# Scan rows ordered so that neighbours on DVE do not depend on each other, statistics aggregated among the rows, and the last stage's weights loaded and folded during the scan

## The chip, the cores and the metric

One NeuronCore of a Trainium2 chip. Its engines each run their own list of instructions in order and wait for one another through semaphores: PE (matrix products and transposes, into the PSUM memory), DVE (vector arithmetic), ACT (scalar engine: copies, scaling, functions; it can also issue DMAs), POOL (a second, slower vector engine without access to PSUM) and SP (issues DMAs). PEld is PE's weight load. The metric is the time on the device of one execution, in microseconds (us).

## The reference

Four layers, each of the form x + f(groupnorm(x)), on x of 4 images x 128 x 128 pixels x 128 channels in float32; a norm group is 4 channels of an image.

```python
x = x + relu(deform_conv(gn(x), w_off, b_off, w_def))     # layer 0: 3x3, bilinear samples
# layer 1: a scan over 128 rows, each row of 128 pixels
def step(carry, row):
    new = row + relu(conv1d_same(carry, W))               # 9 taps, 128 -> 128 channels
    return (new, new)
x = x + scan(step, gn(x))
z = gn(x)                                                 # layer 2
x = x + z @ Wself.T + (sum(z, 2) @ Wm.T)[:, :, None] + (sum(z, 1) @ Wk.T)[:, None]
xn = layer_norm(gn(x))                                    # layer 3: a triangle product
left, right = (xn @ lw + lb) * sigmoid(xn @ lgw + lgb), (xn @ rw + rb) * sigmoid(xn @ rgw + rgb)
out = einsum('bkjd,bkid->bijd', left, right)
x = x + (layer_norm(out) * sigmoid(xn @ ogw + ogb)) @ to_out_w + to_out_b
```

Layer 1 is the serial part: row y + 1 needs the finished row y. Below, x1 is the result of layer 0 and x2 that of layer 1.

## The kernel before

Three stages follow one another: `deform_layer` (layer 0), `scan_layer` (layer 1) and `message_and_triangle` (layers 2 and 3). Inside each main part the order of every engine's list is the order in which the code is written (`manual_schedule`); the framework adds the semaphore waits that the data and the reuse of buffers call for.

**Between layer 0 and the scan.** `deform_layer` ends with what is left of the last convolution, 32 `bn_stats` on the last chunk of x1, the groupnorm factors of the last image (`x1_norm`), and then a flag `far` (L757 to L769): whether any sampling offset left a small window. `ranges` holds the offsets' extremes. After it the program branches on `far`; all five engines read the flag, branch and meet again. The general path isn't taken with these inputs.

**The scan.** The four images go side by side. A row's pixels are split by position modulo 3 into three phases of 43, 43 and 42 columns, and the nine-tap convolution is done as a short convolution over the phases, which saves products: `carry` holds three phases (parts 0 to 2) and three sums of them (parts 3 to 5): 0+1, 1+2, 0+1+2. In each row PE makes the `edge` product (L1081, `pa`: two weights, first with carry part 0, then with part 2), then four products `m1` (part 1), `m01` (part 3), `m12` (part 4) and `m012` (part 5), each in its own PSUM bank, and then it transposes row y + 1 (`turned`, L1061). ACT copies `m1` out of PSUM (L1111) and scales the transposed row with the norm (`scaled`, L1068, `rowT`). DVE then works down one chain: `e = m01 - m1` (L1117), `y0 = edge + e` (L1119), carry part 0 = max(y0, 0) + rowT (L1120), `f = m12 - m1` (L1124), `y2 = f - edge` (L1127), carry part 2 (L1128), `e + f` (L1131), `y1 = m012 - (e + f)` (L1133), carry part 1 (L1134), the three sums of carries (L1141 to L1143), three additions of x1 into `x2c` (L1145), and four `bn_stats`, one for each image (L1150). POOL adds x2 over the rows (`sum_h`, L1148); SP stores four rows at a time to x2T (L1153) and loads four rows of x1 at a time (L1052). PSUM is full: two banks for the transposed rows (`ps_x`), two for the edge products, four for the others.

After the last row DVE computes `sum_w` from the statistics and then aggregates 128 rows of statistics for each image (L1157, `counted`).

**The start of the last stage.** `message_and_triangle` loads its weights: the square matrices and columns on ACT's queue (L1196 to L1230), five bias rows on SP's (L1227, L1231). The norm's gain and the removal of the mean are folded into `wcat`, the 640 columns of all five projections, by two products with `less` and `first` for each of two column blocks (L1244, L1247). Then SP fetches the first two blocks of x2T into `R` (L1342). `prelude(0)` turns `counted` into the group factors (a product with `gmean`, the variance, another product, a square root on ACT at L86, a reciprocal on DVE), and makes the message terms. Then `sums_of(0)` multiplies R into `self_ps` (L1354) and writes `X` (L1365).

Of the kernel before, what the change touches and what calls it, by code (L numbers as in the profile page):

```python
# [9 lines left out]
F32 = mybir.dt.float32  # L10
# [8 lines left out]
P = 128  # L19
B = 4  # L20
# [12 lines left out]
DQ = P // NQ  # L33

# [145 lines left out]
def deform_layer(tc, c, small, x, w_off, b_off, w_def, x1, tabs, offs):  # L180
# [14 lines left out]
    with ExitStack() as ctx:  # L195
# [552 lines left out]
        for _ in convs:  # L748
            pass
        count(len(to_count))  # L750
        beside["norms"].append(x1_norm(B - 1, stats))
        while step(B, S):
            pass


# [4 lines left out]
        nc.vector.scalar_tensor_tensor(most, ends[:, 1:2], -1.0, ends[:, 0:1], ALU.mult, ALU.max)  # L760
        most_ps = ps_g.tile([1, 2 * NL], F32, name="most_ps", tag="gn_ps")
# [7 lines left out]
        nc.vector.tensor_copy(far, row)  # L769
        return norms, far  # L770
# [240 lines left out]
def scan_layer(tc, c, small, x1, w, norms, x2T):  # L1011
# [4 lines left out]
    WP = N + 5  # L1016
    counted = small.tile([P, B, 2], F32, name="counted2")
    sum_w = small.tile([P, B, S], F32, name="sum_w")
    sum_h = small.tile([P, B, S], F32, name="sum_h")
    with ExitStack() as ctx:  # L1020
# [5 lines left out]
        ps_m = ctx.enter_context(tc.tile_pool(name="l1ps_m", bufs=1, space=PSUM))  # L1026

        stats = wp.tile([P, B, S, 6], F32, name="stats2")
# [14 lines left out]

        carry = [wp.tile([P, 2 * PHASES, B, WP], F32, name=f"carry_{i}") for i in range(2)]
# [40 lines left out]

        order = {getattr(mybir.EngineType, e) for e in ("PE", "Activation", "DVE", "Pool", "SP")}
        ctx.enter_context(tc.manual_schedule(engines=order))
        chunks = {0: rows(0), RB: rows(RB)}
        px = turned(0)
        ready = {0: (px, scaled(px))}  # L1090
        add, less = ALU.add, ALU.subtract
        for y in range(S):
# [7 lines left out]
            if y:  # L1100
# [10 lines left out]
                nc.scalar.copy(m1, ps["m1"])  # L1111
            if y + 1 < S:
                pn = turned(y + 1)
                ready[y + 1] = (pn, scaled(pn))
            if y:
                e = two.tile([P, B, N], F32, name="e")
                nc.vector.tensor_tensor(e, ps["m01"], m1, less)  # L1117
                y0 = two.tile([P, B, N], F32, name="y0")
                nc.vector.tensor_tensor(y0, pa[:, :, 0:N], e, add)  # L1119
                nc.vector.scalar_tensor_tensor(  # L1120
# [3 lines left out]
                nc.vector.tensor_tensor(f, ps["m12"], m1, less)  # L1124
                y2 = two.tile([P, B, N], F32, name="y2")
                n2 = COUNT[2]
                nc.vector.tensor_tensor(y2[:, :, 0:n2], f[:, :, 0:n2], pa[:, :, 1 : 1 + n2], less)  # L1127
                nc.vector.scalar_tensor_tensor(  # L1128
                    kept(new, 2), y2[:, :, 0:n2], 0.0, part(rt, 2), ALU.max, add
                )  # L1130
                nc.vector.tensor_tensor(e, e, f, add)  # L1131
                y1 = two.tile([P, B, N], F32, name="y1")
                nc.vector.tensor_tensor(y1, ps["m012"], e, less)  # L1133
                nc.vector.scalar_tensor_tensor(  # L1134
# [5 lines left out]
            if y + 1 < S:  # L1140
                nc.vector.tensor_tensor(kept(new, 3, N), kept(new, 0, N), kept(new, 1, N), add)  # L1141
                nc.vector.tensor_tensor(kept(new, 4, N), kept(new, 1, N), kept(new, 2, N), add)
                nc.vector.tensor_tensor(kept(new, 5, N), kept(new, 3, N), kept(new, 2, N), add)  # L1143
            for p in range(PHASES):
                nc.vector.tensor_tensor(  # L1145
                    x2c[:, :, i, p:S:PHASES], part(px, p), kept(new, p), add
                )
            nc.gpsimd.tensor_tensor(sum_h, sum_h, x2c[:, :, i], add)  # L1148
            for b in range(B):
                nc.vector.bn_stats(stats[:, b, y, :], x2c[:, b, i])  # L1150
# [3 lines left out]
        nc.vector.tensor_tensor(sum_w, stats[:, :, :, 1], stats[:, :, :, 4], add)  # L1154
        nc.vector.tensor_scalar(sum_w, sum_w, S / 2.0, None, ALU.mult)
        for b in range(B):
            nc.vector.bn_aggr(counted[:, b], stats[:, b].rearrange("p n s -> p (n s)"))  # L1157
# [17 lines left out]
def message_and_triangle(tc, c, x2T, x3d, gates, counted, w2, w3, out):  # L1175
# [5 lines left out]
    wself_T, wm_T, wk_T = w2  # L1181
    (norm_g, norm_b, left_w, left_b, right_w, right_b, lgate_w, lgate_b, rgate_w, rgate_b,
     ogate_w, ogate_b, onorm_g, onorm_b, to_out_w, to_out_b) = w3
# [7 lines left out]
    with ExitStack() as ctx:  # L1191
        wp = ctx.enter_context(tc.tile_pool(name="l3w", bufs=1))

        def column(v, name):
            t = wp.tile([P, 1], F32, name=name)
            nc.scalar.dma_start(t, v.rearrange("(p o) -> p o", o=1))  # L1196
            return t

        wself = wp.tile([P, P], F32, name="wself")
        nc.scalar.dma_start(wself, wself_T)  # L1200
        wm = wp.tile([P, P], F32, name="wm")
        nc.scalar.dma_start(wm, wm_T)
        wk = wp.tile([P, P], F32, name="wk")
        nc.scalar.dma_start(wk, wk_T)
        gcol = column(norm_g, "gcol")
        bcol = column(norm_b, "bcol")
        og = column(onorm_g, "og")
        ob = column(onorm_b, "ob")
        outb = column(to_out_b, "outb")
        outw = wp.tile([P, P], F32, name="outw")  # L1210
        nc.scalar.dma_start(outw, to_out_w)

        wcat = wp.tile([P, NW + P], F32, name="wcat")
        with tc.tile_pool(name="l3prep", bufs=1) as prep, tc.tile_pool(
            name="l3ps_w", bufs=2, space=PSUM
        ) as ps_w:
            raw = prep.tile([P, NW + P], F32, name="wraw")  # L1220
            braw = prep.tile([1, NW + P], F32, name="braw")
# [540 lines left out]
```

## Time and profile before

| what | value |
|---|---|
| median of 3 runs | 5691.27 us (5687.96 to 5703.16) |
| the profiled execution | 5688.34 us, its span 5686.6 us |
| layer 0, until the engines branch | 0 to 3336 us |
| branch and start of the scan | 3336 to 3354 us |
| the scan's rows | 3354 to 4098 us |
| end of the scan, prelude | 4098 to 4142 us |
| the last stage | 4142 to 5686 us |
| PE busy over the span | 5214.1 us, 92% |
| DVE busy over the span | 3277.2 us, 58% |
| ACT busy over the span | 2798.5 us, 49% |

How to read it: a line of the timeline gives the start in us, the duration in us, the engine, the line of the code, the operation, what it writes and reads, and how many such instructions were merged. A line of the waits gives who waited for whom, the total in us, how often, and the longest. A line of the busy time by stretches gives the stretch, its length, the busy time of each engine with the number of instructions, the granted clock of PE, the DMA engines' busy share and GB/s. ACTq and SPq are the parts of ACT and SP that issue DMAs; while ACT issues one it does nothing else. The ends of PE's matmuls are modelled, so for PE the starts say more than the ends.

### The profile page before, as it was taken

What the parts mean: (1) busy time and instruction counts of PE and PEld (TensorE: products, weight loads), DVE (VectorE), ACT (ScalarE), POOL (GpSimd) and SP (SyncE); (2) the same over time, 40 slices, a digit from 0 to 9 for tenths busy, and PEclk for the clock granted to TensorE, in tenths of its full rate; (3) what the DMA queues carried; (4) which work ended last, traced back from release to release, by engine and by line L of the source; (5) the groups of instructions that cost most, each with busy time, mean ns of one, the idle gap of its engine ahead of it and who ended that gap; (6) DMA issues with size and microseconds to landing.
All of it is one profiled execution on the core that took longest, in us unless ns stands there. A gap on an engine that the chain in (4) does not pass through costs nothing. (4 is left out here: it accounts for less than half of the span.)

```text
span 5686.6 us, 112077 instructions
## 1 busy us (share of the span) xinstructions
PE 5214.1 (92%) x42401; PEld 4461.0 (78%) x42401; DVE 3277.2 (58%) x10323; ACT 2798.5 (49%) x5890; POOL 780.3 (14%) x674
## 2 busy tenths in 40 slices
PE   2899999999999999999999979999879788798897
PEld 1778888888888888888888879999848568577686
DVE  5544444554444544445433359999974764756756
ACT  1355554455554455555544423333264673764746
POOL 2021211001110011111000002222100200200202
PEclk9899999999999999999999989999989999999999
DMA  4555555556554555555443422222230531623515
GB/s 145 139 138 133 137 125 114 132 123 137 133 137 99 128 135 127 138 120 126 101 82 68 80 60 90 90 90 90 78 150 31 204 145 43 232 90 112 213 42 169
DMA packets 1132346, 671.45 MB, mean 118 GB/s; under 512 B 736461, under 2 KB 1002894, under 8 KB 1113366
## 3 DMA queue, kind: packets, MB, share of 16 engines
q1 hardware_dynamic: 1121650, 657.77, 43.6%
q8 instruction: 338, 5.54, 0.4%
q10 hardware_dynamic: 10148, 6.43, 0.4%
q14 instruction: 210, 1.72, 0.1%
HBM read 382.88 MB, written 281.11 MB: 117 GB/s over the span
## 5 line engine op out<-in xcount | busy, mean ns | idle before, releaser
L509 DVE TENSOR_TENSOR m<-ty,t_ps 120x390 f32<-120x390 f32 x1548 | 804.6, 557 | 1501.6 <-ACT ty L507 1500.4
L520 PEld LDWEIGHTS v_ps<-m,pixels 120*128 120x128 f32 x11352 | 1440.4, 194 | 86.0 <-issue 8.9
L520 PE MATMUL v_ps<-m,pixels 120*128 120x108 f32 (+1 forms) x11352 | 1466.3, 274 | 3.6 <-ACT v L530 3.5
L530 ACT COPY v<-v_ps 128x432 f32<-128x432 f32 x1376 | 718.9, 522 | 1275.8 <-PE v_ps L520 1272.8
L578 PE MATMUL conv_ps<-v,wdef 128*128 128x128 f32 (+2 forms) x5160 | 1304.0, 379 | 6.4 <-DVE x1c L551 5.9
L578 PEld LDWEIGHTS conv_ps<-v,wdef 128*128 128x128 f32 x5160 | 814.6, 193 | 255.8 <-issue 21.4
L507 ACT COPY ty<-t_ps 120x390 f32<-120x390 f32 x1560 | 688.1, 489 | 176.7 <-PE t_ps L497 169.2
L497 PE MATMUL t_ps<-places,spread 25*120 25x99 bf16 (+1 forms) x10836 | 520.4, 260 | 61.1 <-DVE m L509 36.5
L497 PEld LDWEIGHTS <-spread 25*120 25x120 bf16 x10896 | 339.3, 137 | 222.9 <-issue 121.5
L1534 PEld LDWEIGHTS proj_ps<-wcat,X 128*128 128x128 f32 x4096 | 480.2, 194 | 30.0 <-issue 29.0
L1534 PE MATMUL proj_ps<-wcat,X 128*128 128x128 f32 x4096 | 488.9, 278 | 1.7 <-DVE R L1540 0.4
L392 POOL TENSOR_TENSOR off<-off,koff 72x512 f32<-72x512 f32 x128 | 162.0, 1266 | 2295.5 <-DVE off L389 2202.7
L1540 DVE TENSOR_TENSOR L<-proj_ps,work 128x256 f32<-128x256 f32 x256 | 154.6, 604 | 384.8 <-ACT work L1538 384.8
L1068 ACT ACTIVATE rowT<-x1T_ps,t_x,s_x 128x128 f32<-128x128 f32 x512 | 192.7, 457 | 367.5 <-PE x1T_ps L1061 347.2
L1081 PE MATMUL m_ps<-carry,w 128*128 128x172 f32 x2286 | 361.7, 311 | 0.0
L1613 POOL TENSOR_TENSOR work<-work,gate 128x512 f32<-128x512 f32 x128 | 164.2, 1283 | 1417.6 <-ACT work L1612 1165.3
L1081 PEld LDWEIGHTS m_ps<-carry,w 128*128 128x128 f32 x2286 | 346.0, 188 | 0.0
L1148 POOL TENSOR_TENSOR sum_h<-sum_h,x2c 128x512 f32<-128x512 f32 x128 | 162.3, 1268 | 1166.7 <-DVE x2c L1145 1166.7
L1538 ACT ACTIVATE work<-proj_ps 128x512 f32<-128x512 f32 x256 | 151.1, 597 | 311.1 <-PE proj_ps L1534 311.1
L1624 PE MATMUL out_ps<-outw,work 128*128 128x128 f32 x1024 | 193.8, 292 | 34.1 <-POOL work L1613 33.5
L1354 PE MATMUL self_ps<-R,ws 128*128 128x512 f32 x256 | 157.6, 705 | 70.1 <-DVE X L1365 60.9
L1624 PEld LDWEIGHTS out_ps<-outw,work 128*128 128x128 f32 x1024 | 164.8, 203 | 46.8 <-POOL work L1613 46.8
(231 smaller groups left out, 6635.5 us busy)
## 6 DMA issues: line engine op xcount, KB each, us to landing
pixels<-tab SPq DMA_DIRECT2D x688, 123.8 KB
xin<-in_x_dram SPq DMA_DIRECT2D x56, 1024.0 KB
off<-parts SPq DMA_DIRECT2D x64, 891.0 KB
tab<-rows SPq DMA_DIRECT2D x384, 128.0 KB
places<-off SPq DMA_DIRECT2D x688, 55.7 KB
x<-x1c SPq DMA_DIRECT2D x32, 1024.0 KB
x1rows<-x SPq DMA_DIRECT2D x128, 256.0 KB
x2T<-x2c SPq DMA_DIRECT2D x128, 256.0 KB
```

Source lines behind the costliest of these rows:

```text
L497: nc.tensor.matmul(to, lhsT=spread[p0 : p0 + KROWS, ph, :], rhs=mov, start=True, stop=True,)
L507: nc.scalar.copy(ty[:, 0:n], tp[0:LANES, 0, 0:n])
L509: nc.vector.tensor_tensor(m, ty[:, 0:n].rearrange("p (r c) -> p r c", c=PADW), tx, ALU.mult)
L520: nc.tensor.matmul(vp[:, h * n : h * n + rows * w].rearrange("p (k c) -> p k c", c=w), lhsT=pix[0:LANES, xb, :], rhs=m[:, :, RX * xb : RX ...
L530: nc.scalar.copy(v[:, :, c0 : c0 + 4 * RX].rearrange("p k (h c) -> p k h c", c=RX), vp[:, 0 : 4 * n].rearrange("p (h k c) -> p k h c", h=4 ...
L578: nc.tensor.matmul(pc[:, at : at + r1 - r0, :], lhsT=wdef[:, 3 * ky + kx, :], rhs=v[:, k0 + kx, r0:r1, kx : kx + S], start=m == 0, stop=m ...
L1068: nc.scalar.activation(rt[:, b, :], px[:, b, :], AF.Identity, bias=t, scale=s)
L1081: nc.tensor.matmul(to, lhsT=wgt, rhs=src[:, :, at : at + n], start=i == 0, stop=i + 1 == len(todo),)
L1148: nc.gpsimd.tensor_tensor(sum_h, sum_h, x2c[:, :, i], add)
L1534: nc.tensor.matmul(pp[:, j], lhsT=X[:, j0 + j, :], rhs=wcat[:, cols], start=True, stop=True)
L1613: nc.gpsimd.tensor_tensor(a, a, gt, ALU.mult)
L1624: nc.tensor.matmul(po[:, j], lhsT=a[:, j], rhs=outw, start=False, stop=True)
```

## The change

Four things change.

1. **The order of DVE's instructions in a scan row.** The four `bn_stats` of a row are no longer at its end: they are queued, and the next row places one behind each of `e`, `y0`, `f` and the first sum of carries. The `e + f` step moves ahead of carry part 2, and the three additions into `x2c` and the three sums of carries stand between the other steps.
2. **The statistics of x2 are aggregated among the rows.** The statistics tile holds two chunks of 16 rows. Once a chunk is full, the next rows aggregate it with one DVE instruction a row: one `bn_aggr` for each image, then `sum_w`'s part. After the last row the eight partial means and variances are combined by seven small instructions.
3. **The last stage's weights.** Loads and folding move into the scan. The loads, 19 of them (the bias rows as well), are issued on ACT's queue before the first `scaled`; POOL prepares `less`, `first` and `gained` in row 4 (DVE did so before); PE makes the products in rows 8 and 10 into a third tile of the two-bank pool `ps_x`; ACT copies them out (DVE before) and POOL adds the biases. The first two blocks of R are fetched by SP in rows 65 and 67, into a buffer that now lives through both stages.
4. **The flag.** The extremes are reduced before the last convolution's remainder, and the flag is computed before the last `bn_stats` and the last norm of layer 0.

```diff
@@ deform_layer
-        for _ in convs:
-            pass
-        count(len(to_count))
-        beside["norms"].append(x1_norm(B - 1, stats))
-        while step(B, S):
-            pass
         ends = wp.tile([2 * NL, 2], F32, name="ends")
...
         nc.vector.scalar_tensor_tensor(most, ends[:, 1:2], -1.0, ends[:, 0:1], ALU.mult, ALU.max)
+        for _ in convs:
+            pass
         most_ps = ps_g.tile([1, 2 * NL], F32, name="most_ps", tag="gn_ps")
...
         nc.vector.tensor_copy(far, row)
+        count(len(to_count))
+        beside["norms"].append(x1_norm(B - 1, stats))
+        while step(B, S):
+            pass
@@ scan_layer
-        stats = wp.tile([P, B, S, 6], F32, name="stats2")
+        prep = ctx.enter_context(tc.tile_pool(name="l1prep", bufs=1))
+        stats = wp.tile([P, 2, B, CH, 6], F32, name="stats2")
+        parts_of = wp.tile([P, B, NCH, 2], F32, name="parts2")
...
+        def count(n):
+            for _ in range(min(n, len(to_count))):
+                nc.vector.bn_stats(*to_count.pop(0))
+
+        def summed(ch, i):
+            if ch < 0:
+                return
+            now = stats[:, ch % 2]
+            if i < B:
+                nc.vector.bn_aggr(parts_of[:, i, ch], now[:, i].rearrange("p n s -> p (n s)"))
+            to = sum_w[:, :, ch * CH : (ch + 1) * CH]
+            if i == B:
+                nc.vector.tensor_tensor(to, now[:, :, :, 1], now[:, :, :, 4], add)
+            if i == B + 1:
+                nc.vector.tensor_scalar(to, to, S / 2.0, None, ALU.mult)
...
         chunks = {0: rows(0), RB: rows(RB)}
+        later.load(prep)
         px = turned(0)
         ready = {0: (px, scaled(px))}
...
+            if y in (2 * RB, 2 * RB + 2):
+                px2 = ps_x.tile([P, B, S], F32, name="x1T_ps")
+                later.product((y - 2 * RB) // 2, px2.rearrange("p b s -> p (b s)"))
             if y + 1 < S:
                 pn = turned(y + 1)
                 ready[y + 1] = (pn, scaled(pn))
...
                 nc.vector.tensor_tensor(e, ps["m01"], m1, less)
+                count(1)
                 y0 = two.tile([P, B, N], F32, name="y0")
                 nc.vector.tensor_tensor(y0, pa[:, :, 0:N], e, add)
+                count(1)
...
                 nc.vector.tensor_tensor(f, ps["m12"], m1, less)
+                count(1)
...
+                nc.vector.tensor_tensor(e, e, f, add)
                 nc.vector.scalar_tensor_tensor(
                     kept(new, 2), y2[:, :, 0:n2], 0.0, part(rt, 2), ALU.max, add
                 )
-                nc.vector.tensor_tensor(e, e, f, add)
                 y1 = two.tile([P, B, N], F32, name="y1")
                 nc.vector.tensor_tensor(y1, ps["m012"], e, less)
+                summed_up(0)
                 nc.vector.scalar_tensor_tensor(
                     kept(new, 1), y1, 0.0, part(rt, 1), ALU.max, add
                 )
...
+            summed_up(2)
+            kept_sum(3, 0, 1)
+            count(1)
+            kept_sum(4, 1, 2)
+            summed_up(1)
+            kept_sum(5, 3, 2)
             nc.gpsimd.tensor_tensor(sum_h, sum_h, x2c[:, :, i], add)
-            for b in range(B):
-                nc.vector.bn_stats(stats[:, b, y, :], x2c[:, b, i])
+            to_count.extend(
+                (stats[:, y // CH % 2, b, y % CH, :], x2c[:, b, i]) for b in range(B)
+            )
...
+            summed(y // CH - 1, y % CH)
+            if y == RB:
+                later.fold(prep)
+            if y in (S // 2 + 1, S // 2 + 3):
+                i = (y - S // 2) // 2
+                nc.sync.dma_start(later.R[i], x2T[0, :, i * DQ : (i + 1) * DQ, :])
-        nc.vector.tensor_tensor(sum_w, stats[:, :, :, 1], stats[:, :, :, 4], add)
-        nc.vector.tensor_scalar(sum_w, sum_w, S / 2.0, None, ALU.mult)
-        for b in range(B):
-            nc.vector.bn_aggr(counted[:, b], stats[:, b].rearrange("p n s -> p (n s)"))
+        count(B)
+        for i in range(B + 2):
+            summed(NCH - 1, i)
+        kept_means, kept_vars = parts_of[:, :, :, 0], parts_of[:, :, :, 1]
+        mean, var = counted[:, :, 0], counted[:, :, 1]
+        nc.vector.tensor_reduce(mean, kept_means, AX.X, add)
...
+        nc.vector.tensor_scalar(var, var, 1.0 / NCH, None, ALU.mult)
@@ last_weights (new; the loads, the folding and the products of message_and_triangle)
+    def load(prep):
+        w.wself, w.wm, w.wk = square(wself_T, "wself"), square(wm_T, "wm"), square(wk_T, "wk")
+        w.outw = square(to_out_w, "outw")
+        w.gcol, w.bcol = column(norm_g, "gcol"), column(norm_b, "bcol")
+        w.og, w.ob, w.outb = column(onorm_g, "og"), column(onorm_b, "ob"), column(to_out_b, "outb")
...
+        for n, (wgt, bias) in enumerate(both):
+            nc.scalar.dma_start(blocks[:, :, n, :], wgt.rearrange("p (q e) -> p q e", q=NQ))
+            nc.scalar.dma_start(
+                bblocks[:, :, n, :], bias.rearrange("(o q e) -> o q e", o=1, q=NQ)
+            )
+        nc.scalar.dma_start(w.raw[:, WCAT - P :], ogate_w)
+        nc.scalar.dma_start(w.braw[:, WCAT - P :], ogate_b.rearrange("(o n) -> o n", o=1))
+
+    def fold(prep):
+        w.less = prep.tile([P, P], F32, name="less")
+        nc.gpsimd.tensor_copy(w.less, c.ident)
...
+        nc.gpsimd.tensor_scalar(w.gained, w.raw, w.gcol, None, ALU.mult)
+
+    def product(part, pw):
+        at = slice(512 * part, min(512 * (part + 1), WCAT))
+        n = at.stop - at.start
+        nc.tensor.matmul(pw[:, :n], lhsT=w.less, rhs=w.gained[:, at], start=True, stop=False)
+        nc.tensor.matmul(pw[:, :n], lhsT=w.first, rhs=w.raw[:, at], start=False, stop=True)
+        nc.scalar.copy(w.wcat[:, at], pw[:, :n])
+        nc.gpsimd.tensor_tensor(w.wcat[0:1, at], w.wcat[0:1, at], w.braw[:, at], ALU.add)
```

`summed_up(p)` is the addition of phase p into `x2c`, `kept_sum` one of the sums of carries. The loads, the folding and the first two fetches of R in `message_and_triangle` are removed.

## The prediction

> **What bounds the kernel now.** I read the page first (three stages: deformed convolution, scan, messages and triangle), then the busy time by stretches, to see which engine is full in the scan that the change rewrites.
>
> ```profile
> core 0: us, PE busy (x) PEld busy (x) DVE busy (x) ACT busy (x) POOL busy (x), PEclk, DMA share, GB/s
> 3600.00:3700.00 100.00, 100.00 (x689) 99.86 (x689) 94.07 (x326) 30.93 (x86) 21.55 (x17) 1.00 0.28 85
> 4090.00:4140.00 50.00, 13.46 (x59) 10.70 (x58) 30.49 (x65) 2.10 (x6) 2.53 (x2) 0.63 0.26 90
> ```
>
> In the scan PE and its weight loads are full at a granted clock of 1.00, and DVE is nearly full. At 4090 to 4140, the change of stage, PE stands. Next, who waits inside the scan, and one row in order of time:
>
> ```profile
> POOL sum_h L1148 <- DVE x2c L1145: 574.2, 125, 8.9
> ACT rowT L1068 <- PE x1T_ps L1061: 344.4, 124, 3.2
> DVE e L1117 <- PE m_ps L1081: 4.3, 1, 4.3
> ```
> ```profile
> 3703.49 0.34 DVE L1117 TENSOR_TENSOR e<-m_ps,m 128x172 f32<-128x172 f32 x1
> 3705.26 0.40 DVE L1128 SCALAR_TENSOR_TENSOR carry<-y,rowT 128x168 f32<-128x168 f32 x1
> 3706.21 0.94 PEld L1081 LDWEIGHTS edge_ps<-carry,wconv 128*128 128x128 f32 x6
> 3706.38 0.40 DVE L1134 SCALAR_TENSOR_TENSOR carry<-y,rowT 128x172 f32<-128x172 f32 x1
> 3707.07 0.33 DVE L1142 TENSOR_TENSOR carry<-carry 128x172 f32<-128x172 f32 x1
> 3707.11 0.93 PEld L1081 LDWEIGHTS m_ps<-carry,wconv 128*128 128x128 f32 x6
> 3707.31 0.33 DVE L1143 TENSOR_TENSOR carry<-carry 128x172 f32<-128x172 f32 x1
> 3708.15 2.85 PE L1081 MATMUL m_ps<-carry,w 128*128 128x172 f32 x18
> 3709.32 0.34 DVE L1117 TENSOR_TENSOR e<-m_ps,m 128x172 f32<-128x172 f32 x1
> ```
>
> A row takes 3709.32 - 3703.49 = 5.83 us. PE never appears as a waiter: its 40 matmuls of a row follow one another with no gap. The carries it needs are done before it asks: carry 2 (L1128) ends at 3705.66 and is wanted at 3706.21; carry 1 (L1134) ends at 3706.78 and is wanted at 3707.11. So PE sets the row, and DVE, although it looks as full, follows. Last, the chain that ended last, at the two changes of stage:
>
> ```profile
> 4098.32 2.32 DMA x2T<-x2c
> 4100.64 14.04 DVE counted L1157 x4
> 4122.52 0.63 ACTq L1230
> 4123.20 0.30 ACT std_x L86
> 4131.93 7.33 DMA R<-x2T
> 4139.51 5.08 PE self_ps L1354 x6
> ```
>
> Here everything is in series: 14 us of aggregation, the weight loads' issues on ACT with the square root behind them, then the weights' product and the fetch of R.
>
> **The change part by part**, against the profiled execution (5688.34 us; the median of the runs is 2.9 us above it).
>
> **The row on DVE.** An instruction that reads the one before starts 0.37 us after it; an independent one 0.25 (L1142 to L1143: 3707.07, 3707.31), 0.31 behind a scalar_tensor_tensor, 0.20 behind a bn_stats. The new order has no neighbours that depend: e 0; stat 0.25; y0 0.45; stat 0.70; carry 0 at 0.90; f 1.21; stat 1.46; y2 1.66; e+f 1.91; carry 2 at 2.16, done 2.56; y1 2.47; x2c 2.72; carry 1 at 2.97, done 3.37; x2c, sum, stat, sum, x2c, sum: free at 4.73. DVE's row falls from 5.83 to about 4.7, but its next e still waits for PE's product. What the row costs is whether PE is fed: carry 2 is wanted at 2.72 and done at 2.56 (before: 2.17), carry 1 wanted at 3.62 and done at 3.37 (before 3.29). Slack falls from 0.55 to 0.16 us and from 0.33 to 0.25; a wake takes 0.04 to 0.05. I take 0 us for 127 rows. The cover is that 0.1 us; if it is gone, each 0.1 us costs 127 x 0.1 = 12.7 us. A gain is excluded but for what gaps PE's stream may hide: 40 matmuls at the shortest spacings (0.107 for a transpose, 0.145 for 172 columns) would be 5.65, so at most 0.18 a row.
>
> The rule of the Trainium skill (VectorE: DVE Perf Modes, section "The DRAIN you can't avoid") speaks against this change: the next DVE instruction does not start until the pipeline is empty, semaphore or not (the section names an exception for one that nothing holds back). The rows above differ, 0.25 against 0.37. By the rule every step would cost its duration, carry 2 would end near 3.6 and PE would wait 0.9 us a row, some 119 us in all. I go by the rows.
>
> The aggregation adds, for each 16 rows, four bn_aggr and two small instructions, one a row: 0.25 to 0.45 us in DVE's spare 1.1.
>
> **The weights' loads, 19 of them, on ACT's queue ahead of the first rowT.** DVE's first copies wait for rowT, and PE's first product for those. In the prelude 14 such issues took 4114.76 to 4123.15, 0.60 each. From 3342.0 that is 11.4 us, to 3353.4, against 3350.83 now: +2.6, the lower end. The upper end is the program's start, where ACT's queue issued 27 loads from 0.81 to 33.73, 1.22 each, because some stood until earlier transfers had landed:
>
> ```profile
> 6.01 0.84 ACTq L235 DMA_DIRECT2D tab<-zero  x2
> 6.89 0.95 ACTq L240 DMA_DIRECT2D off<-zero  x1
> 12.29 0.81 ACTq L241 DMA_DIRECT2D off<-zero  x1
> ```
>
> That gives 23.2 us, +14.4. I take +7: four issue at once, the rest stand behind the landings of wconv and the first x1rows (3347.5 to 3348.5 by PE's first transposes), then 15 x 0.60. It is nearer the lower end because these transfers are as small as the prelude's.
>
> The skill's rule (DMA: Bandwidth & Descriptors, "Issuing engines are not separate DMA queues") calls the issue usually small beside the transfer. Here ACT's issues are the wait: 29.9 us of idle time before std_x end with them. By the rule this term would be near 0 and the total near -28.
>
> **The products in rows 8 and 10** go into PE's full stream. 512 columns in four passes of 0.43 (172 columns take 0.149) are 1.7 us, and the next transposes then wait for the copy of that bank (0.6, as ACT's 128x512 row of 597 ns) and two wakes: 2.5. The 128-column part: 0.43 + 0.3 + 0.2, 1.0. Together +3.5; bounds 2.2 (passes alone) and 7 (the transposes wait for the row's last x2c). POOL's folding in row 4, six instructions below 1.6 us each (1.27 for 512 columns), lies in its 4.57 idle us a row and is wanted 23 us later. R's two fetches on SP in rows 65 and 67 cost two issues of 0.3 to 0.5 us, ahead of the next x1rows, which is wanted two rows on; DMA share is 0.28. Both cost nothing; without that cover, a few us once.
>
> **The end of the scan.** Before: the last x2c ends at 4097.93, the first X at 4141.60 starts: 43.7 us. After: four stats 0.9; four bn_aggr of 96 values 0.45 each (between 7.51/32 = 0.235 for 48 and 14.05/4 = 3.51 for 768), 1.8; two small sums 0.45; seven dependent small instructions of 0.23 (L160), 1.6; together 4.75. Then the prelude without its cover of loads: mean to variance 1.7; square root to the end of three message products 3.3 (4123.20 to 4125.94, and one product of 0.6 more); z and its sums 1.1; sum product 0.4; first product to first X 2.1 (4139.51 to 4141.60): 8.6. In all 13.4, so -30.3 (27 to 32, by 0.1 us on each of some 30 steps). R lies there already. Next late would be X's space: the last x2T store has landed by 4102, in time.
>
> **The flag moved ahead of the last norm.** L757 to L769 take 1.8 us at the end of DVE's list (3333.74 to 3335.55); the last three come back ahead of the 32 stats with PE's product, 0.65. DVE reaches the branch 1.15 us earlier; bounds -0.6 and -2.3 (if the other engines' 1.4 us of joining is then past). I take -1.2.
>
> **Sum:** 0 + 7 + 3.5 - 30.3 - 1.2 = -21.0: 5667.3 for the profiled execution, 5670 on the scale of the median.
>
> **The rivals.** A: PE must wait a little for carry 2 or carry 1, 0.05 to 0.15 us a row: +6 to +19, 5676 to 5689. For it: the slack of 0.16. Against: seven of nine steps up to carry 2 are spaced as rows show.
> B, slower: the same wait at one place, L1128's carry 2 before the second half of the edge product, grown by an extra wait in front of the interleaved bn_stats. It decides from 21.0/127 = 0.165 us a row, that is carry 2 done at 2.84 instead of 2.56; at 0.3 us it gives 5708. For it: three bn_stats now stand ahead of carry 2. Against: they read a row that was finished 1.2 us before.
> C: the loads wait less and the rows shorten by a few hundredths: 5654 to 5662.
> D: the end gives half, because X or PE waits for something that the old prelude hid: 5685. Against: the store's landing above.
> That DVE was the bound and the row falls to 4.7 (-140 us) would need a wait of PE for DVE, and there is none.
>
> **How the numbers follow.** Forecast 0.70, own range 5662 to 5679 by the ends of its terms; A 0.12, B 0.08, C 0.05, D 0.05. Two runs of this kernel can be told apart from about 0.3%, 17 us: faster means below 5674.2. The forecast lies there four times in five (0.56), C wholly (0.05): 0.61. Within: the rest of the forecast, most of A and D: 0.28. Slower 0.11. The range 5661 to 5687 leaves out B, half of C and little else.
>
> **What would show it.** Right: row period 5.83 still, DVE waiting for PE at e in every row; ACT's first rowT at about 3357; two gaps of PE in rows 8 and 10; 13 to 14 us from the last x2c to the first X. Wrong: a period above 5.9 with a wait of PE for carry; rowT first at 3365; a wait of X's first write for a DMA.

## The result and the profile after

| | before | after |
|---|---|---|
| median | 5693.17 us (5687.96 to 5703.16, 4 runs) | 5660.92 us (5654.38 to 5661.23, 4 runs) |
| the profiled execution, its span | 5688.34, 5686.6 us | 5660.90, 5659.2 us |

The ratio is 0.9938 with a 95% interval of 0.9922 to 0.9954: 32 us faster. The same two kernels were timed again later, together with others on one chip (the second measurement): 5691.76 us (11 runs) and 5669.56 us (5 runs), ratio 0.9960 (0.9944 to 0.9975), 22 us faster. The prediction was 5670 us with a range from 5661 to 5687. The first median lies 0.08 us below that range, the second within 1 us of the forecast, so the question is not only which term was wrong but also why two measurements of one change differ by 10 us.

The tables below cut each profile into the same seven stages, from the start times of the instructions named: to the start of the last x1c; from there to the issue of wconv's load (the end of layer 0 and the branch, "join"); to the first rowT; to the first copy of a row on DVE; to the end of the last x2c (the scan's rows); to the first X (the end of the scan); to the end.

| stage, us | before | after | difference | after, second measurement | predicted |
|---|---|---|---|---|---|
| layer 0, to the last x1c | 3318.16 | 3314.92 | -3.2 | 3316.37 | 0 |
| last x1c to wconv (join) | 23.40 | 19.41 | -4.0 | 19.41 | -1.2 |
| wconv to first rowT | 9.27 | 16.87 | +7.6 | 16.37 | +7 |
| first rowT to first copy | 1.53 | 1.54 | 0.0 | 1.54 | 0 |
| first copy to last x2c | 745.56 | 749.65 | +4.1 | 748.22 | +3.5 |
| last x2c to first X | 43.67 | 12.96 | -30.7 | 12.97 | -30.3 |
| first X to the end | 1545.02 | 1543.82 | -1.2 | 1549.05 | 0 |
| span | 5686.6 | 5659.2 | -27.4 | 5663.9 | -21.0 |

The stages that the change touches sum to -23.0 us (second measurement -24.9); the two that it does not touch moved by -4.4 us in the first and by +2.2 us in the second.

The busy time by stretches of the kernel after, with the same columns as before:

```profile
core 0: us, PE busy (x) PEld busy (x) DVE busy (x) ACT busy (x) POOL busy (x), PEclk, DMA share, GB/s
3600.00:3700.00 100.00, 100.00 (x689) 99.83 (x688) 83.42 (x334) 30.98 (x86) 21.69 (x17) 1.00 0.28 85
4090.00:4140.00 50.00, 36.43 (x121) 19.12 (x119) 40.03 (x156) 17.65 (x45) 3.81 (x3) 0.86 0.26 100
```

In the scan PE is as full as before, with the same 689 products in 100 us, and DVE has gone from 94.07 to 83.42 us. At the change of stage all engines work earlier. The waits of the kernel after inside the scan (who waits for whom, total, times, longest):

```profile
ACT rowT L1072 <- PE x1T_ps L1065: 343.0, 125, 3.0
DVE e L1151 <- PE m_ps L1085: 130.7, 127, 5.0
```

The second line is the new one: it stood there once before and stands there in all 127 rows now. One row of the kernel after in order of time shows it as idle time in brackets:

```profile
3701.45 0.34 DVE L1151 TENSOR_TENSOR e<-m_ps,m 128x172 f32<-128x172 f32 x1 [1.11 <-PE m_ps L1085]
3701.70 0.28 DVE L1094 BATCH_NORM_STATS2 stats<-x2c 128x6 f32<-128x128 f32 x1
3703.31 0.33 DVE L1165 TENSOR_TENSOR e<-e,f 128x172 f32<-128x172 f32 x1
3703.55 0.38 DVE L1166 SCALAR_TENSOR_TENSOR carry<-y,rowT 128x168 f32<-128x168 f32 x1
3704.16 0.94 PEld L1085 LDWEIGHTS edge_ps<-carry,wconv 128*128 128x128 f32 x6
3704.36 0.38 DVE L1172 SCALAR_TENSOR_TENSOR carry<-y,rowT 128x172 f32<-128x172 f32 x1
3705.07 0.93 PEld L1085 LDWEIGHTS m_ps<-carry,wconv 128*128 128x128 f32 x6
3707.27 0.34 DVE L1151 TENSOR_TENSOR e<-m_ps,m 128x172 f32<-128x172 f32 x1 [1.11 <-PE m_ps L1085]
```

From e to e it is 5.82 us; the median over all rows is 5.827 us before and after. Carry 2 (L1166) is done at 3703.93, 2.48 us after e, and PE loads the weights for the product that reads it at 3704.16. DVE then waits 1.11 us for PE. PE itself waits for no carry; the only waits for another engine that the profile lists for it in the rows are for ACT's copies of the last weights in rows 8 and 10 (0.7 us the longer one). The end of the scan, from the chain of the kernel after:

```profile
4102.42 0.87 DVE stats L1094 x4
4103.30 1.83 DVE parts L1101 x4
4108.48 0.30 ACT std_x L87
4109.97 0.80 PE msg_ps L1365 x2
4112.81 0.59 PE sum_ps L1377 x2
4113.40 3.54 PE self_ps L1409 x4
```

The 14 us of aggregation, the issues on ACT ahead of the square root, the weights' product and the fetch of R are gone from it; what is left is 1.83 us for the last chunk and the dependent small steps.

### The profile page after: what moved, and what is told of

It reads as the page before. It is cut to its first block, busy times and chain, and to the rows that moved or that the text cites. A ratio compares the mean times of both kernels' runs of the same rounds, so it can differ in the third digit from the quotient of the medians.

```text
span 5659.2 us, 112097 instructions
## 1 busy us (share of the span) xinstructions
PE 5208.6 (92%) x42401; PEld 4459.8 (79%) x42401; DVE 3181.3 (56%) x10362; ACT 2800.7 (49%) x5892; POOL 786.5 (14%) x682
```

## The experiments

Every one is one profiled execution cut into the stages above, unless runs are named. Stages in us:

| kernel | to last x1c | join | to first rowT | rows | end of scan | first X to end |
|---|---|---|---|---|---|---|
| before | 3318.16 | 23.40 | 9.27 | 745.56 | 43.67 | 1545.02 |
| after | 3314.92 | 19.41 | 16.87 | 749.65 | 12.96 | 1543.82 |
| flag_only | 3320.82 | 19.57 | 8.32 | 745.01 | 42.98 | 1550.97 |
| order_only | 3315.85 | 23.60 | 8.21 | 744.63 | 42.76 | 1543.18 |
| agg_only | 3317.92 | 22.38 | 9.04 | 745.22 | 31.45 | 1547.88 |
| weights_only | 3312.33 | 23.01 | 16.27 | 747.72 | 25.11 | 1539.03 |
| old_order | 3318.39 | 19.58 | 16.57 | 764.73 | 12.97 | 1538.73 |
| delay_2 | 3317.25 | 19.62 | 16.76 | 786.93 | 12.97 | 1554.67 |
| fill_2 | 3318.08 | 19.54 | 17.07 | 749.89 | 13.32 | 1533.98 |
| loads_late | 3326.08 | 19.60 | 8.23 | 749.00 | 12.97 | 1549.31 |
| loads_products_late | 3320.59 | 19.53 | 8.46 | 745.26 | 13.18 | 1550.04 |

The rows' stage holds one row that differs from profile to profile for a reason of its own, the first. PE's granted clock is 0.5 at the join and goes to 1.00 only while that row runs: at 3359.0 us in the kernel before, whose first row begins at 3352.76 and takes 8.81 us, and at 3357.0 us in the second profile of the kernel after, whose first row begins at 3354.01 and takes 7.24 us. Over the twelve profiles the first row (from PE's first weight load of one row to that of the next) takes 7.18 to 8.81 us, and that is 5.82 us plus 0.96 of the time lost to the clock in it ((1 - granted clock) x duration, 1.4 to 3.1 us) to within 0.01 us. Without it the rows take 736.75 us before, 741.00 and 740.98 after.

### What the flag is worth: flag_only

The kernel before with one block moved:

```diff
-        for _ in convs:
-            pass
-        count(len(to_count))
-        beside["norms"].append(x1_norm(B - 1, stats))
-        while step(B, S):
-            pass
...
+        for _ in convs:
+            pass
         most_ps = ps_g.tile([1, 2 * NL], F32, name="most_ps", tag="gn_ps")
...
         nc.vector.tensor_copy(far, row)
+        count(len(to_count))
+        beside["norms"].append(x1_norm(B - 1, stats))
+        while step(B, S):
+            pass
```

> The kernel before with one part of the change: the flag is worked out ahead of the last norm. The stretch from the last x1c to the issue of wconv, 23.4 us before and 19.4 us in the changed kernel, tells. Theory: SyncE and GpSimd read the flag some 13 us earlier and are through the branch while VectorE still counts, so that only VectorE's own way is left; the whole 4.0 us come back with this part alone, 19.4 us here. Rival (the prediction): only the 1.2 us by which VectorE reaches the branch earlier come back, 22.2 us, and the rest of the 4.0 us belongs to other parts. The rows, the loads and the end of the scan stay as before: rows of 5.83 us, 9.3 us from wconv to the first rowT, 43.7 us from the last x2c to the first X. Sum by the theory: -4 us.

Measured: 19.57 us, -3.8 of the 4.0, and less than 1 us in each of the three stages behind it that the whole change touches. The theory holds. The table confirms it: the four profiles with the flag in its old place take 22.4 to 23.6 us there, the eight with the new place 19.4 to 19.6. The time line of the kernel before at the join (start, duration, engine, line, operation):

```profile
3333.61 0.21 DVE L90 TENSOR_SCALAR t_x<-gf_mvp,s_x 128x1 f32<-128x1 f32 x1
3335.41 0.14 DVE L769 CAST far<-most_row 1x1 int32<-1x1 f32 x1
3341.56 0.44 ACTq L1030 DMA_DIRECT2D wconv<-in_w_conv_dram  x1
```

The same place of the kernel after:

```profile
3330.70 0.21 DVE L91 TENSOR_SCALAR t_x<-gf_mvp,s_x 128x1 f32<-128x1 f32 x1
3334.33 0.46 ACTq L1033 DMA_DIRECT2D wconv<-in_w_conv_dram  x1
```

Before, DVE's last work ends at 3335.55 and wconv is issued 6.0 us later; after, at 3330.91 and 3.4 us later. So 2.6 us of the gain lie behind DVE's last instruction, and only the rest, 1.4 us, is DVE's shorter list. The trace's records of loads and branches say what the 6.0 us were: before, all five engines read the flag at 3335.57 to 3335.59, and their next record behind the branch comes at 3339.7 to 3340.3; GpSimd and SyncE then step through a row of further semaphores until 3341.1. After, GpSimd and SyncE read the flag at 3315.73, have branched and passed those semaphores at 3321.0, while DVE counts, and only PE, ACT and DVE branch late (at 3329.7 to 3331.3, next record at 3333.1 to 3334.2). The Trainium skill (Runtime: NRT & Kernel Launch, section "Instruction fetch mechanics") says that a taken branch to a place outside the instructions already fetched has to fetch them first. The records agree in kind: 2.7 to 4.1 us stand behind each compare-and-branch. What an engine does in that time no run here shows.

The 2.6 us have three parts. From DVE's first record behind the branch to the issue of wconv it is 1.28 us before and 0.10 after, since GpSimd and SyncE have done their steps by then: 1.2 us. DVE's compare-and-branch is followed by its next record after 4.08 us before and 2.90 after (ACT's after 3.52 and 2.68): 1.2 us more. And DVE reads the flag 0.04 us behind its last instruction before, 0.20 us ahead of the end of that instruction after: 0.2 us. Why the branch is shorter when GpSimd and SyncE have passed it earlier stays open.

### What the new order is worth: order_only and old_order

order_only is the kernel before with the sequence of DVE's row alone; the statistics go into the next row, but are kept whole and aggregated at the end as before.

```diff
+                count(1)
                 y0 = two.tile([P, B, N], F32, name="y0")
...
-            for b in range(B):
-                nc.vector.bn_stats(stats[:, b, y, :], x2c[:, b, i])
+            to_count.extend((stats[:, b, y, :], x2c[:, b, i]) for b in range(B))
```

> The kernel before with the new order of VectorE's row alone (the statistics kept whole and aggregated at the end). Theory: PE sets the row, 5.83 us as before, VectorE now waits about 1.1 us for PE at e in every row, and the scan (745.6 us) and its end (43.7 us) stay within 1 us: the order by itself gains nothing. Rival: part of PE's row is a wait for VectorE that the records do not show, and the row shortens, by up to 0.18 us, 23 us in all.

Measured: a median row of 5.827 us, rows 744.63 us in sum, end 42.76 us. The order by itself gains nothing: without the first row the rows take 737.0 us, against 736.75 before. Its waits in the scan:

```profile
DVE e L1132 <- PE m_ps L1081: 138.2, 126, 1.1
```

DVE has 1.1 us to spare in each row, and the row does not shorten: PE sets it.

old_order is the kernel after with the old sequence of the row:

```diff
                 nc.vector.tensor_tensor(e, ps["m01"], m1, less)
-                count(1)
                 y0 = two.tile([P, B, N], F32, name="y0")
...
-            to_count.extend(
-                (stats[:, y // CH % 2, b, y % CH, :], x2c[:, b, i]) for b in range(B)
-            )
+            for b in range(B):
+                nc.vector.bn_stats(stats[:, y // CH % 2, b, y % CH, :], x2c[:, b, i])
```

> The changed kernel with VectorE's row in the order of before (neighbours depend on each other, the four statistics of a row at its end); aggregation among the rows, weights and flag as changed. Theory: in the old order VectorE has almost nothing to spare in a row, so the 7 x (4 x 0.45 + 0.45), about 15.7 us, of aggregation among the rows show in the time, less what carry 1's 0.33 us of slack takes in: the scan is 8 to 16 us longer than in the changed kernel, in the rows that hold an aggregation. Then the new order is what pays for the aggregation, although by itself it gains nothing. Rival: the old order hides the aggregation as well, the scan is within 2 us, and the new order is worth nothing at all.

Measured: rows of 764.73 us, 15.1 us more than after (16.5 without the first row), at the upper end of what the theory gave. A stretch of the chain of old_order, over two of the rows that hold an aggregation:

```profile
3464.19 0.54 DVE stats L1175 x3
3464.79 0.28 DVE stats L1175
3465.06 0.49 DVE parts L1101
3465.55 0.20 DVE e L1142
3470.40 0.53 DVE stats L1175 x3
3470.99 0.28 DVE stats L1175
3471.27 0.49 DVE parts L1101
3471.76 0.20 DVE e L1142
```

No PE stands in this chain: DVE goes from the statistics to the aggregation to the next e without a wait, and from e to e it is 6.21 us. The six rows of a chunk that hold its aggregation take 2.4 us more in PE's row times, seven chunks 16.6 us; in the rows after them DVE's e follow one another in 5.77 us, 0.06 below PE's 5.83. That 0.06 us was all that DVE had to spare in the old order. So the new order is worth 15 us, but only together with the aggregation among the rows, for which it makes the room. In the old order that aggregation costs the rows more than the 12.2 us that it takes from the end (agg_only, below).

### The two halves of the end: agg_only and weights_only

agg_only is the kernel before with the new row and the aggregation among the rows; weights_only is the kernel before with loads, folding and fetches of R moved into the scan, and nothing else.

```diff
-        stats = wp.tile([P, B, S, 6], F32, name="stats2")
+        stats = wp.tile([P, 2, B, CH, 6], F32, name="stats2")
+        parts_of = wp.tile([P, B, NCH, 2], F32, name="parts2")
...
+            summed(y // CH - 1, y % CH)
```

```diff
         chunks = {0: rows(0), RB: rows(RB)}
+        later.load(prep)
...
+            if y == RB:
+                later.fold(prep)
+            if y in (S // 2 + 1, S // 2 + 3):
+                i = (y - S // 2) // 2
+                nc.sync.dma_start(later.R[i], x2T[0, :, i * DQ : (i + 1) * DQ, :])
```

> The kernel before with the new order of the row and the aggregation among the rows; flag and last weights as before. Theory: the rows stay at 5.83 us; from the last x2c to the first X 43.7 - 11.6, about 32 us, since VectorE is done 5.1 us instead of 16.7 us after the last x2c and the weights' issues, the root and the fetch follow as before. Rival: the issues of the weights' loads wait for something else than the aggregation (the last x2T stores, the scan's space), and the stretch falls by less than 6 us, to 38 us or more.

> The kernel before with the weights loaded ahead of the first row, folded in rows 4, 8 and 10, and the two fetches of R in rows 65 and 67; order of the row, aggregation and flag as before. Theory: the parts add up: from the last x2c to the first X 43.7 - 19, about 24.7 us (30.6 less the 11.6 of the aggregation); from wconv to the first rowT 16.9 us instead of 9.3; rows 8 and 10 together 3.5 us longer. Rival: with the aggregation in its old place the loads were hidden behind it or the parts overlap: the stretch at the end falls by less than 15 or by more than 23 us.

Measured: 31.45 and 25.11 us from the last x2c to the first X, against 43.67 before: -12.2 and -18.6, in sum -30.8, and the kernel after has -30.7. The parts add up. agg_only keeps its rows (745.22 us); weights_only has the later first rowT (16.27 us), and rows 8 and 10 together 3.5 us longer (8.32 and 6.84 instead of 5.83). Its rows as a whole are only 2.2 us longer than before, because its first row is 1.6 us shorter; without the first row they are 3.8 us longer.

### How near carry 2 is: delay_2 and fill_2

Two spare bn_stats a row in the kernel after, ahead of carry 2 in the one, at the end of DVE's row in the other:

```diff
                 nc.vector.tensor_tensor(e, e, f, add)
+                for _ in range(2):
+                    nc.vector.bn_stats(spare, rt[:, 0, :])
                 nc.vector.scalar_tensor_tensor(
                     kept(new, 2), y2[:, :, 0:n2], 0.0, part(rt, 2), ALU.max, add
                 )
```

```diff
             kept_sum(5, 3, 2)
+            for _ in range(2):
+                nc.vector.bn_stats(spare, rt[:, 0, :])
```

> The changed kernel with two spare bn_stats (0.28 us each, of a row that is long ready, into a place that nobody reads) put directly ahead of carry 2 in every row. VectorE's list stays shorter than the row (4.7 + 0.57 = 5.3 of 5.83 us), but carry 2 and all behind it come 0.57 us later. Theory (what counts is when carry 2 is there, and its slack after the change is about 0.23 us): PE waits 0.57 - 0.23 = 0.34 us in each row, the row is 6.1 to 6.25 us and the scan 35 to 53 us longer. Rival (PE sets the row as long as VectorE's work fits in it): the row stays at 5.83 us and the time within 3 us.

> The changed kernel with the same two spare bn_stats at the end of VectorE's row, behind the last sum, where no carry of this row stands behind them. Theory: VectorE's wait for PE at e falls from 1.11 us a row to 0.4 to 0.6 us and the row stays at 5.83 us: 0 to 2 us on the whole. Rival (VectorE's added work shows wherever it stands, as in the old order): the row grows by 0.2 us or more, 25 us or more.

Measured: with the delay a median row of 6.133 us, rows 37.3 us longer in sum; with the filling a median row of 5.827 us and rows 0.2 us longer. The same work at two places of the same list costs 37 us or nothing. The waits of delay_2 in the scan, where PE in the kernel after waits for no carry:

```profile
DVE e L1152 <- PE m_ps L1086: 95.7, 120, 3.6
PEld edge_ps L1086 <- DVE carry L1169: 37.5, 118, 0.5
```

and of fill_2, where DVE's wait falls to 0.6 us in the 85 rows that still have one, and PE waits for a carry once, 0.2 us:

```profile
DVE e L1152 <- PE m_ps L1086: 52.6, 85, 4.6
```

L1169 is carry 2. In one row of delay_2 in order of time the two spare instructions, the late carry and the wait stand one behind the other:

```profile
3703.63 0.62 DVE L1168 BATCH_NORM_STATS2 spare<-rowT 128x6 f32<-128x128 f32 x2
3704.17 0.38 DVE L1169 SCALAR_TENSOR_TENSOR carry<-y,rowT 128x168 f32<-128x168 f32 x1
3704.60 0.90 PEld L1086 LDWEIGHTS edge_ps<-carry,wconv 128*128 128x128 f32 x6 [0.32 <-DVE carry L1169]
```

The carry came 3704.17 - 3703.63 = 0.54 us later and the row grew by 0.31, so the slack of carry 2 in the kernel after is 0.23 us. The wait that rival B of the prediction priced is thus real, at the place that was named, but it took added work to make it; the change stops 0.23 us short of it.

### Can the price of the loads and products be avoided: loads_late and loads_products_late

The 19 loads go one a row into rows 5 to 23, the folding into row 32; in loads_late the two products go into rows 36 and 38, in loads_products_late behind the last row:

```diff
                 ready[y + 1] = (pn, scaled(pn))
+            if y > RB:
+                later.issue(1)
...
-            if y == RB:
+            if y == 8 * RB:
                 later.fold(prep)
```

```diff
-            if y in (2 * RB, 2 * RB + 2):
-                px2 = ps_x.tile([P, B, S], F32, name="x1T_ps")
-                later.product((y - 2 * RB) // 2, px2.rearrange("p b s -> p (b s)"))
...
+        for part in range(2):
+            px2 = ps_x.tile([P, B, S], F32, name="x1T_ps")
+            later.product(part, px2.rearrange("p b s -> p (b s)"))
         count(B)
```

> The changed kernel with its 19 loads of the last weights issued one a row on ScalarE's queue in rows 5 to 23, behind rowT, instead of ahead of the first rowT; the folding in row 32 and the products in rows 36 and 38. Theory: from wconv to the first rowT 9.3 us instead of 16.9; an issue of 0.6 us fits in ScalarE's four idle microseconds of a row, so rows 5 to 23 stay at 5.83 us; rows 36 and 38 cost the 3.5 to 4.1 us that rows 8 and 10 cost. Sum -7.6 us against the changed kernel. Rival: an issue stands behind the landing of an earlier transfer, m1 and rowT behind it come late, and the 19 rows give back 4 us or more.

> The changed kernel with the loads in rows 5 to 23, the folding in row 32, and both products of the last weights behind the last row, where PE stands while VectorE aggregates. Theory: -8 us ahead of the first rowT and -4.1 us in the rows, while the end stays at 13.0 us because 2.4 us of PE's passes and their copies lie beside the 5 us of statistics: -12 us against the changed kernel, in the stages that this touches (from wconv to the first X 769 us instead of 781). Rival: the copies and sums of the products stand ahead of the square root and of the message's products, and the end grows by 2 to 4 us, which takes half of the 4.1 us back. The whole time, if the unchanged stages stay the same: 5649 us.

> The changed kernel again, beside the one with late loads and products, on the same chip: 0.9938 of the time before (0.9922 to 0.9954); its own stages as in its first profile (16.9 us from wconv to the first rowT, 749.6 us of rows, 13.0 us at the end), and 12 us more than the kernel with late loads and products. The two stages that no part of the change touches (up to the last x1c, and from the first X on) have differed by 6 us and more from one kernel to the next, so whole times are told apart only by rounds.

Measured in the stages: loads_late has its first rowT 8.23 us after wconv, 8.6 us earlier than the kernel after; rows 5 to 23 stay at 5.83 us, and rows 36 and 38 take 8.44 and 6.85 (row to row at e), as rows 8 and 10 do in the kernel after. Its time as a whole, 5668.45 us, is 7.5 us above that of the kernel after, because its two untouched stages are 16.7 us longer; a single time would have hidden the gain. loads_products_late has 8.46 us to the first rowT, no long row there (745.26 us) and 13.18 us at the end: from wconv to the first X 768.4 us, against 781.0 in the first profile of the kernel after and 779.1 in its second.

Measured in time, in the second measurement: 5659.99 us (5653.51 to 5661.81, 6 runs) against 5669.56 (5665.65 to 5670.69, 5 runs) of the kernel after. All six lie below all five; the medians differ by 9.6 us. Against the kernel before the ratio is 0.9941 (0.9927 to 0.9955). It is the fastest of the three kernels there; the 12 us expected were 10. Two expectations missed: 5649 us for this kernel (5659.99) and a ratio of 0.9938 for the kernel after (0.9960). In the profiles the two untouched stages take 11.9 and 6.7 us more than in the first profile of the kernel after, which is what both counted on.

How an issue on ACT costs, in the kernel after ahead of the first row (time line):

```profile
3336.23 0.52 ACTq L1246 DMA_DIRECT2D wk<-in_wk_T_dram  x1
3338.33 0.33 ACTq L1246 DMA_DIRECT2D outw<-in_to_out_w_dram  x1
3340.98 0.34 ACTq L1241 DMA_DIRECT2D gcol<-in_norm_g_dram  x1
3343.21 0.34 ACTq L1241 DMA_DIRECT2D og<-in_onorm_g_dram  x1
3346.53 0.59 ACTq L1263 DMA_DIRECT2D wraw<-in_right_w_dram  x1
3350.84 0.30 ACTq L1268 DMA_DIRECT2D braw<-in_ogate_b_dram  x1
3351.20 2.91 ACT L1072 ACTIVATE rowT<-x1T_ps,t_x,s_x 128x128 f32<-128x128 f32 x8 [20.73 <-DMA wraw<-in_rgate_w_dram]
```

The records also say what three of the issues stand for. Those of outw, gcol and og wait for semaphores that the first, second and fourth load of x1rows raise as well; these loads have landed whole at 3338.31, 3340.96 and 3343.19, and each of the three issues starts 0.02 us later.

and in loads_late, in a row (time line), where the issue lies between two parts of rowT and no engine is held up:

```profile
3393.23 0.46 ACT L1072 ACTIVATE rowT<-x1T_ps,t_x,s_x 128x128 f32<-128x128 f32 x1 [2.78 <-PE x1T_ps L1065]
3393.24 0.33 ACTq L1248 DMA_DIRECT2D wm<-in_wm_T_dram  x1
3396.89 0.34 DVE L1153 TENSOR_TENSOR e<-m_ps,m 128x172 f32<-128x172 f32 x1 [1.10 <-PE m_ps L1085]
```

The text ahead of the prediction says that ACT does nothing else while it issues. This row shows otherwise: the part of rowT that began at 3393.23 runs on beside the issue, to 3393.69. Only the next part starts behind the issue, at 3393.58. DVE's wait of 1.10 us for PE is that of every row.

## Why the prediction was right or wrong

**The row, 0 us: right.** It is 5.827 us before and after, PE waits for no carry, and DVE waits at e, as the prediction said it would be seen. Carry 2 was expected 2.56 us after e with 0.16 us of slack; it comes at 2.48, and delay_2 puts the slack at 0.23. The rule weighed there (the Trainium skill, VectorE: DVE Perf Modes, section "The DRAIN you can't avoid") would have put carry 2 near 3.6 us and cost 119 us (the durations alone sum to 3.3 us; 3.6 needs the 0.03 us more by which dependent neighbours follow each other). In the row shown, the statistic starts 0.25 us after e began, while e itself takes 0.34. Neighbours that do not depend on each other overlap here; that goes with the exception that the section names, and the measurement decides.

**The loads, +7 us: right.** +7.6 and +7.1 us. The first three follow one another, outw, gcol and og stand 1.4 to 2.3 us each before their issue, behind landings of x1rows, and from left_w on the rest follow at about 0.6 us each. The prediction had one stand of about 4 us there; it is three, of 5.3 us together. (The program's start, from which it took the upper end, issues mostly writes of zeros, not loads.) The other rule weighed (DMA: Bandwidth & Descriptors, section "Issuing engines are not separate DMA queues"), by which this would be near nothing, does not describe this place: moved among the rows the same issues cost nothing, and ahead of the first row 8 us.

**The products, +3.5 us: right.** From e to e row 8 became 2.61 us longer and row 10 1.02 (2.5 and 1.0 predicted), and PE's next transposes stand 0.7 us for ACT's copy, as the sum had it. Three later rows are 0.14 us longer each on PE, in agg_only too. The sum of the scan grew by 4.1 us in the first measurement and by 2.7 in the second; the 1.4 us between them are the first row's, and without it both are 4.2.

**The end of the scan, -30.3 us: right.** -30.7 in both profiles, and its two parts, -12.2 and -18.6, stand alone.

**The flag, -1.2 us with bounds -0.6 and -2.3: wrong, and this is the step that failed.** The direction and DVE's share were right (1.15 predicted, 1.4 measured). What failed is the cost behind DVE's last instruction. The prediction read it as "the other engines' 1.4 us of joining", put its fall at nothing in the forecast, and its outer bound does not even hold all of it (1.15 + 1.4 would be 2.55). What fell there is 2.6 us: the joining (1.2 us) and also the branch itself, which the prediction had left as long as it was. flag_only shows the 3.8 us alone. The step missed 2.8 us; the range's lower end, set from such bounds, was 1.7 us too high for this reason alone.

**What is not in the prediction at all: the untouched stages.** With all its terms measured the touched stages give -23.0 us, 5665.3 us against the profiled execution, 5668 on the scale of the median. The first measurement gave 5660.92, the second 5669.56. The remainder is in layer 0 and in the last stage, where both kernels do the same work. Over the twelve profiles of this study layer 0 took 3312 to 3326 us and the last stage 1534 to 1555 us, whatever was changed in the scan. Where a sum of terms is 21 us, a range whose lower end lies 9 us below the forecast has no room for that. Neither of the two carried the first time out of the range alone: with the flag at -1.2 it would have been 5663.7 us, with the untouched stages as before 5665.3, both inside. That the second measurement hits the forecast is luck: its touched stages gave 3.9 us more than predicted, and the rest made up for it.

The rivals: A and B did not occur, C gave the right time for a wrong reason (its loads that wait less and shorter rows are not there), D did not occur.

## What to carry to other kernels

Work that an engine does off the bound is free only by its place: the same two instructions cost 37 us ahead of the carry that PE wants next and nothing behind the last one, so look up which result is wanted first and how late it may be. Making room on an engine that is not the bound gains nothing by itself, but it can pay for work taken from a stretch in series (15 us here), so judge the two edits together. And measure small terms by stages: the touched stages repeat within 1 or 2 us, the untouched ones wander by 14 to 21.

## What the runs showed of the hardware that was not expected

The wandering of the untouched stages goes with PE's granted clock. The trace records each change of that clock; summed over a stage, the time lost to it (as above) was 68 to 79 us in layer 0 and 83 to 102 us in the last stage. Over the twelve profiles the length of the stage and the time lost in it have a correlation of 0.87 in layer 0 and 0.85 in the last stage, with slopes of 0.92 and 0.94: a microsecond lost to the clock goes with nearly a microsecond of time. Taking the lost time off leaves 4.6 of the 13.8 us by which layer 0 varies and 9.9 of the 20.7 us of the last stage, so it is a part and not the whole. That the clock is the cause was not tried; what makes it differ from one execution to the next stays open.

It does not settle why the two measurements of the kernel after do not overlap (5654.38 to 5661.23 and 5665.65 to 5670.69 us). Their granted clocks, 0.9670 and 0.9658 on average over the runs, would put about 7 us between them, but each run's clock is recorded to a thousandth, which is 5.7 us; and the two profiles go the other way: the second lost 2.4 us less to the clock in the two untouched stages and took 6.7 us longer in them. That stays open.

The branch on the flag costs each engine 2.7 to 4.1 us before and after, and those that can read the flag early pass it beside other work. The bn_aggr of 96 values takes 0.577 us from start to end (0.49 us until the next instruction starts in the old order), and four of 768 values took 3.56 us each before: the aggregation is paid by the value here, so cutting it into chunks costs little: eight chunks at 0.46 us (1.83 / 4, from start to start) are 3.7 us, one of 768 values 3.51 (14.04 / 4).
